# Seven products of quarters for layer 0's output projection, from the second image on

## The chip, the cores and the metric

The kernel runs on one core of a Trainium2 chip. A core has a matrix engine (TensorE, PE in the profile, with the weight loads listed apart as PEld), a vector engine (VectorE, DVE), a scalar engine (ScalarE, ACT), a general engine (GpSimd, POOL) and a sync engine (SyncE, SP) that issues most DMA transfers. Each engine works through its own instructions in the order in which they were written out, and waits where an operand is not ready. Matrix results land in PSUM, everything else that is on the chip lies in SBUF, and the rest in DRAM.

The metric is the device time of one execution in microseconds (us). The kernel before takes 2559.91 us, the median of three runs (2559.35 to 2560.78).

## The reference

Two attention layers follow one another on x of shape (8, 512, 32, 32): eight images, 512 channels, 1024 positions. Everything is fp32 outside of what is shown.

```python
# layer 0, per image, T = 1024
h = group_norm(x, gn_w, gn_b)                      # 32 groups
qkv = einsum('oc,bct->bot', qkv_w, h) + qkv_b      # 8 heads of 64 channels
q, k, v = fake_quant(q), fake_quant(k), fake_quant(v)   # 8 bits, one range for all images
w = softmax(einsum('bct,bcs->bts', q * scale, k * scale))
a = einsum('bts,bcs->bct', w, v).reshape(b, 512, T)
a = einsum('oc,bct->bot', proj_w, a) + proj_b      # the projection
x1 = x + a
# layer 1, one head of 512 channels, T = 1024
h = group_norm(x1, gn_w, gn_b)
q, k, v = (h^T @ w + bias for w in (wq, wk, wv))
out = softmax(q k^T / sqrt(512)) v
x2 = x1 + out @ wp + bp
```

The line that the change touches is the projection of layer 0: for each image a product of a 512x512 weight with 512x1024 values, then a bias for each output channel and the residual x.

## The kernel before, in words

Channels lie on the 128 partitions in four chunks (`CC = 4`), the 1024 positions in two halves of 512 (`NH = 2`). The eight heads of layer 0 are worked in four pairs.

Up to about 400 us the group norm and the products for q, k and v of all images run, since the ranges for the quantisation cover all of them. From then on two streams are woven together. `attention()` (line 1018) does layer 0's attention for image after image, in units of (image b, pair j, half hf, key tile s): a unit has two score products (`st<-q,k`), an exponential on ACT into a tile `pt` (four buffers, so unit u reuses the buffer of unit u - 4), a cast of it to 16 bit (`two`, by ACT, or by POOL for every fourth), a subtract on DVE that keeps the rest in a second 16-bit tile (`two<-pt,two`), the product with the values (`av<-two,v`, first with the cast part and then with the rest) and the sums of the rows (`sm<-two,ones`). At the end of a pair `finish` copies the products and sums out of PSUM and `divide` scales the values into a tile `ao`, of 128x2x512 for each pair, so four of these make the projection's right-hand side.

The other stream, `others()` (line 1900), does for one image after the other the projection, the second group norm (`norm1`, line 1344) and layer 1 (`layer1`, line 1655). It is one image behind the attention, and each `yield` in it lets the attention go on by four units. So while layer 1 of image b runs, the attention of image b + 1 runs beside it and ends shortly before the projection that needs it; the projection and norm of image b + 1 stand inside layer 1 of image b, behind the fourth of the seven products of its last `o_run` (line 1540; `first()` at line 1764 calls `project(b + 1, score_bank)`). For the last image no attention is left to run beside.

The order on DVE and ACT is written out by a planner. The class `InOrder` (line 53) wraps both engines. Its `do` puts an operation down at once; its `later` puts one on a list of chores with a cost, a time when it is ready and a time when it is due; `fill` takes chores from the list as long as they fit before a given time by the planner's own clock, the one that is ready first going first; and `settle` takes all of a kind at once. A `dma_start` on ACT adds 0.5 us to the planner's clock. Each instruction is tied behind the one put down before it on its engine. All operations of DVE and ACT are therefore recorded at line 91 (`call` in `InOrder`), and all matmuls at line 209 (`mm`), so that the tiles' names tell them apart: `pj` is the projection's PSUM tile, `wp` its weight, `h` the residual x that becomes x1, `vec` the biases.

Before each projection `load_wp` (line 1265) loads its weight of 1 MB in one DMA and `load_x2` loads x in two, all issued on ACT's queue near the end of layer 1 of the image before (lines 1756 and 1757). `project` (line 1296) then takes, in each half and for each of four output chunks, four matmuls of 128x512 into one PSUM bank; DVE evicts each bank with one operation that adds bias and residual, SP stores x1, and `bn_stats` and `bn_aggr` gather the statistics of the second group norm (chores "pj", forced at the end by `settle("pj")`). Between the halves there is one `yield`, in which the attention goes on.

Most of the products of layer 1 are already done by `seven` (line 1393): two matrices of 2x2 quarters are multiplied with seven products of quarters in place of eight, after sums and differences of the quarters were made on both sides. Here a product of quarters is four matmuls of 128x256, and its result goes with others into two PSUM banks that are used in turn. The sums of the weights' quarters are made once, those of the values for each image and half. Tiles of layer 1 that the change borrows are `vsum` (sums of the value tile's quarters, needed by `o<-g,vsum`), and `v` (`vt`, the value tile itself, 128x8x512).

Of the kernel before, what the change touches and what calls it, by code (L numbers as in the profile page):

```python
# [9 lines left out]
F32 = mybir.dt.float32  # L10
# [8 lines left out]
P = 128  # L19
# [39 lines left out]
def attn_pair_kernel(  # L59
# [97 lines left out]
    def elements(n):  # L157

        return 0.21 + n * 0.957e-3

    def chore():
        dve.fill(pe.t)

    def awaits(t):

        pe.t = max(pe.t, t + 0.1)
# [140 lines left out]
    with ExitStack() as fast:  # L307
# [710 lines left out]
        def attention():  # L1018
# [138 lines left out]
            def finish(b, j, hf, u):  # L1157

                nm = f"{b}_{j}"
                if hf == 0:  # L1160
                    if b:
                        settle("ao")
                    ao[b, j] = aop.tile([P, NH, 512], F32, tag="ao", name=f"ao_{nm}")
                    if b == 0 and j % 2 == 1:
                        rss[b, j] = kept_u[:, 0:2].rearrange("p h k n -> p h (k n)")
                    else:
                        rss[b, j] = l1p.tile([P, NH, 512], F32, tag="rs", name=f"rs_{nm}")
                aot, rs = ao[b, j], rss[b, j]
                act.do(0.6, lambda: act.copy(aot[:, hf, :], avs.pop((b, j, hf))))
                act.do(0.6, lambda: act.copy(rs[:, hf, :], sms.pop((b, j, hf))))  # L1170
                if hf == 0:
                    return
                del rss[b, j]
                n = b * PAIRS + j

                apart = small.tile([P, 2, 16], F32, tag="apart", name=f"apart_{nm}")
                for w in range(2):
                    nc.sync.dma_start(
                        apart[:, w, :],
                        rs[2 * w * QUAD : 2 * (w + 1) * QUAD : QUAD].rearrange(  # L1180
                            "r h (p k) -> r h p k", k=16
                        ),
                    )

                def divide():
                    dve.scalar_tensor_tensor(aot, aot, scl[:, 2:3], rs, ALU.mult, ALU.mult)

                def spread():
                    r = rcs[:, n * 16 : (n + 1) * 16]
                    dve.tensor_add(r, apart[:, 0, :], apart[:, 1, :])  # L1190
                    dve.reciprocal(r, r)
                    nc.sync.dma_start(rs_d[n].rearrange("r (p k) -> (r p) k", k=16), r)
                    for i, r in enumerate(HALF):
                        nc.sync.dma_start(
                            rs[r], rs_d[n][2 * i : 2 * i + 2, :].partition_broadcast(CH)
                        )
                    if InOrder.planned:
                        dve.later("ao", elements(1100), divide, dve.t + 7.0, 20.0)
                    else:
                        dealt.append((u + (20 if j < PAIRS - 1 else 13), "ao", divide))  # L1200

                if InOrder.planned:
                    dve.later("ao", 0.4, spread, pe.t + 5.0, 8.0)
                else:
                    dealt.append((u + (12 if j < PAIRS - 1 else 7), "ao", spread))
# [58 lines left out]
                dma(xts[b][:, :, bass.ts(hf, 512)], x_v[b, :, :, bass.ts(hf, 512)])  # L1264

        def load_wp(b, dma):
            wps[b] = l2p.tile([P, CC, C], F32, tag="sums", name=f"wp0_{b}")
            dma(wps[b], w_sq[WP0])

        def load_first(u):  # L1270

# [21 lines left out]
            for t, src in zip(wm_tiles(b), wm_d):  # L1293
                act.dma_start(t, src)

        def project(b, bank=bank):

            settle("ao")  # L1300
            st, mvs[b] = stat_tiles(CC, f"b{b}")
            wp0 = wps.pop(b)
            for hf in range(NH):
                for oc in range(CC):
                    ps = bank(f"pj_{b}_{hf}_{oc}")
                    for cc in range(CC):
                        mm(
                            ps, lhsT=wp0[:, cc, bass.ts(oc, P)], rhs=ao[b, cc][:, hf, :],
                            start=(cc == 0), stop=(cc == CC - 1),
                        )  # L1310
                    xx = xts[b][:, oc, bass.ts(hf, 512)]

                    def evict():
                        dve.scalar_tensor_tensor(
                            xx, ps, vec[:, V_PB0 + oc : V_PB0 + oc + 1], xx, ALU.add, ALU.add
                        )
                        nc.sync.dma_start(x1_d[b][oc // 2][hf][:, oc % 2, :], xx)

                    def stats(oc=oc, hf=hf, xx=xx):
                        dve.bn_stats(st[:, oc, hf, :], xx)  # L1320
                        if hf == NH - 1:
                            aggregate(mvs[b], st, oc)

                    dve.do(elements(550), evict)
                    dve.later("pj", 0.62 + 0.2 * hf, stats, within=4.0)
                    chore()
                if hf + 1 < NH:
                    yield -1
            settle("pj")
            for k in [k for k in ao if k[0] == b]:  # L1330
                del ao[k]
# [12 lines left out]
        def norm1(b, bank=bank):  # L1344

            def at(cc, hf):
                return xts[b][:, cc, bass.ts(hf, 512)]

            def put(hf, cost, work):
                if hf == 0:  # L1350
                    dve.do(cost, work)
                else:
                    dve.later("h", cost, work, within=27.0)

            def put_sum(hf, i, work):
                if hf == 0:
                    dve.later("t4" if i == 3 else "t", elements(512), work, within=10.0 + 2.0 * i)
                else:
                    put(hf, elements(512), work)

            for n, _ in enumerate(norm_steps(
                at, at, V_GN1W, bank, f"b{b}", put=put, mv=mvs[b]
            )):
                if n == 2:
                    sums[b] = l2p.tile(
                        [P, 3, NH, CC // 2, 256], F32, tag="sums", name=f"sums2_{b}"
                    )
                    for hf in range(NH):
                        h11, h12, h21, h22 = quarters(b, hf)
                        t1, t2, t4 = (sums[b][:, i, hf] for i in range(3))  # L1370
                        for i, args in enumerate((
                            (t1, h12, h11), (t2, h22, t1), (h12, h22, h12), (t4, h21, t2)
                        )):
                            put_sum(hf, i, lambda args=args: tt(*args, ALU.subtract))
                yield
# [14 lines left out]
            dve.later("o", 0.25, spread, pe.t + 4.0, 5.0)  # L1390
            return rs

        def seven(nm, pairs, keep, whole, add, bank=bank):

            nonlocal turn
            turn ^= 1  # L1400
            x, y = (bank(f"{nm}_{i}").rearrange("p (t n) -> p t n", t=2) for i in range(2))

            def product(n, ps, start):
                left, right = pairs[n]
                k = left.shape[1]
                for t in range(2):
                    for i in range(k):
                        mm(
                            ps[:, t, :], lhsT=left[:, i, bass.ts(t, P)], rhs=right[:, i, :],
                            start=start and t == 0 and i == 0, stop=(i == k - 1),  # L1410
                            skip_group_check=True,
                        )

            work = (
                (0, x, True, keep, 0), (1, y, True, add, 0), (2, x, False, keep, 1),
                (3, y, True, keep, 2), (4, x, False, add, 2), (6, y, False, add, 1),
                (5, x, False, whole, None),
            )
            for i, (n, ps, start, out, m) in enumerate(work):
                awaits(free[(i + turn) % 2])  # L1420
                product(n, ps, start)
                free[(i + turn) % 2] = out(ps) if m is None else out(m, ps)
                yield i + 1

        free = [0.0, 0.0]
        turn = 0

        def slots(gq):
# [226 lines left out]
        def layer1(b, steps):  # L1655
# [46 lines left out]
            for hf in range(NH):  # L1702
# [52 lines left out]
                if last and b + 1 < B:  # L1755
                    load_wp(b + 1, act.dma_start)
                    load_x2(b + 1, act.dma_start)
                if done >= B:
                    load_x1(b, hf, 0, 1, rx, aop)
                settle("v")  # L1760
                between = [lambda: iter((1,)), lambda: iter(()), lambda: iter(())]
                if b + 1 < B and last:

                    def first():
                        nonlocal ahead
                        yield -1
                        yield from project(b + 1, score_bank)
                        yield 2
                        ahead = norm1(b + 1, score_bank)
                        next(ahead)  # L1770
# [534 lines left out]
```

## Time and profile before

| what | value |
|---|---|
| median of three runs | 2559.91 us |
| the profiled execution | 2559.32 us |
| its span | 2557.2 us |
| granted TensorE clock | 0.999 |
| busy: PE | 2515.9 us, 98% |
| busy: DVE | 1897.6 us, 74% |
| busy: ACT | 1346.5 us, 53% |
| busy: POOL | 186.0 us, 7% |
| matmul records of the projection | 512 |
| first start of a projection, images 0 to 7 | 692.7, 930.72, 1171.0, 1411.2, 1651.4, 1891.9, 2132.3, 2362.4 us |

A line of the profile's groups gives the line of the kernel, the engine, the operation, the output tile and the tiles read, their shapes, the number of instructions, their busy time and mean duration in ns, and after the bar the idle time of the engine just before them with what ended most of it. A line of the timeline gives the start, the duration, the engine, and the same names; a group of equal instructions that follow one another is one line, `x32` being their number, and what stands in square brackets is how long the engine was idle before and what it waited for. The durations of matmuls are modelled and overlap: 32 matmuls that follow one another are read from the start of the first to the start of what comes next on PE. One fp32 matmul is recorded twice. A queue such as ACTq or SPq lists the issue of DMA transfers. The chain of work that ended last is followed back from the last instruction; its line gives the share of the span that each engine holds of it.

### The profile page before, as it was taken

To read this page: it belongs to the slowest core of one execution; us is meant where nothing else is said; L and a number is where in the kernel's file an instruction comes from. 1 tells how busy PE (TensorE), PEld (TensorE's weight loads), DVE (VectorE), ACT (ScalarE), POOL (GpSimd) and SP (SyncE) were. 2 spreads that over 40 slices of the span, in tenths; PEclk is the share of its full clock that TensorE was granted. 3 is DMA by queue.
4 is the path that set the end of the run, shared out by engine and by line. 5 is a ranking of instruction groups with operands and counts; after the bars stand their busy time and mean duration, and the time that the engine had idled before them with its cause. 6 is when DMAs were issued, how large, how long until landed. Compare 5 with 4: busy or idle time off the path is not lost.

```text
span 2557.2 us, 38727 instructions
## 1 busy us (share of the span) xinstructions
PE 2515.9 (98%) x15670; PEld 1746.2 (68%) x15670; DVE 1897.6 (74%) x2747; ACT 1346.5 (53%) x1685; POOL 186.0 (7%) x167
## 2 busy tenths in 40 slices
PE   8999999999999999999999999999999999999998
PEld 4788888873357756775777577667756775777787
DVE  7887776668887778777877787777778777885544
ACT  3332223319857655665666466656655665664121
POOL 0000000001100001000100100010101000100000
PEclk9999999999999999999999999999999999999999
DMA  4533333236622232223313222322232123212211
GB/s 168 177 142 125 131 124 122 109 131 162 162 88 63 79 116 85 58 74 122 98 57 100 92 79 78 110 92 63 79 112 88 55 71 128 96 42 80 87 38 39
DMA packets 160717, 250.70 MB, mean 98 GB/s; under 512 B 27152, under 2 KB 93712, under 8 KB 159120
## 3 DMA queue, kind: packets, MB, share of 16 engines
q1 hardware_dynamic: 125792, 182.81, 21.6%
q10 hardware_dynamic: 30560, 57.71, 6.5%
q0 software_dynamic: 4176, 7.60, 1.7%
q8 instruction: 125, 2.05, 0.3%
q14 instruction: 64, 0.52, 0.1%
HBM read 153.64 MB, written 86.28 MB: 94 GB/s over the span
## 4 chain that ended last, share of the span: by engine, by line
PE 85%; DVE 5%; ACT 2%; issue 1%; DMA 1%; POOL 0%; SPq 0%; ACTq 0%; DVEq 0%
PE s L209 15%; PE o L209 13%; PE qkps L209 12%; PE pj L209 8%; PE av L209 8%; PE v2ps L209 7%; PE vps L209 6%; PE g L209 6%; PE st L209 4%; PE sm L209 3%; DVE two L91 2%; ACT pt L91 1%; PE fold L209 1%; DVE h L91 1%; DVE acc L91 0%
## 5 line engine op out<-in xcount | busy, mean ns | idle before, releaser
L91 ACT ACTIVATE pt<-st,esc 128x1024 f32<-128x1024 f32 x467 | 496.4, 1114 | 332.1 <-PE st L209 317.6
L91 DVE TENSOR_TENSOR two<-pt,two 128x1024 f16<-128x1024 f32 x467 | 561.5, 1216 | 131.0 <-POOL two L1092 100.7
L91 ACT CAST two<-pt 128x1024 f16<-128x1024 f32 x346 | 350.8, 1055 | 6.9 <-ACT p L91 5.1
L1092 POOL CAST two<-pt 128x1024 f16<-128x1024 f32 x112 | 146.0, 1304 | 1409.4 <-PE sm L209 746.3
L209 PE MATMUL av<-two,v 128*32 128x512 f16 x3968 | 245.9, 381 | 2.5 <-DVE two L91 2.1
L209 PE MATMUL s<-g,h 128*128 128x256 f32 x1024 | 233.4, 380 | 0.0
L209 PE MATMUL pj<-ao,wp 128*128 128x512 f32 x512 | 224.1, 595 | 0.6 <-DVE h L91 0.6
L209 PEld LDWEIGHTS s<-g,h 128*128 128x128 f32 x1024 | 192.9, 190 | 31.0 <-issue 4.3
L91 ACT ACTIVATE u_ring<-qkps,qkbt 128x512 f32<-128x512 f32 x89 | 60.9, 685 | 243.8 <-PE qkps L209 219.3
L209 PEld LDWEIGHTS <-v 128*32 128x32 f16 x3968 | 91.8, 96 | 140.0 <-issue 66.7
L209 PEld LDWEIGHTS pj<-ao,wp 128*128 128x128 f32 x512 | 96.0, 190 | 122.5 <-issue 110.8
L209 PE MATMUL s<-g,sums 128*128 128x256 f32 x768 | 178.4, 381 | 0.2 <-DVE p L91 0.2
L209 PE MATMUL o<-p,v 128*128 128x256 f32 x768 | 175.2, 382 | 1.0 <-DVE p L91 1.0
L209 PE MATMUL st<-q,k 64*128 64x512 bf16 x1024 | 163.4, 382 | 11.9 <-ACT pt L91 7.5
L209 PEld LDWEIGHTS o<-p,v 128*128 128x128 f32 x768 | 144.3, 190 | 27.1 <-issue 5.7
L209 PEld LDWEIGHTS s<-g,sums 128*128 128x128 f32 x768 | 144.7, 190 | 24.2 <-issue 4.6
L209 PE MATMUL sm<-two,ones 128*32 128x512 f16 x1984 | 136.0, 379 | 0.0
L209 PEld LDWEIGHTS <-k 64*128 64x128 bf16 x1024 | 34.8, 94 | 143.8 <-issue 142.2
L209 PE MATMUL qkps<-half,w_high 128*128 128x512 f32 x480 | 132.4, 398 | 0.0
L209 PE MATMUL qkps<-half,w_mix 128*128 128x512 f32 x480 | 130.6, 394 | 1.0 <-DVE half L91 1.0
L209 PE MATMUL qkps<-half,w_low 128*128 128x512 f32 x480 | 130.5, 394 | 0.0
L209 PE MATMUL v2ps<-wm,h 128*128 128x256 f32 x512 | 119.9, 383 | 1.9 <-ACT g L91 1.3
(226 smaller groups left out, 3902.2 us busy)
## 6 DMA issues: line engine op xcount, KB each, us to landing
rs<-rs_d SPq DMA_DIRECT2D x76, 256.0 KB
x<-in_x_dram SPq DMA_DIRECT2D x32, 512.0 KB
q_d<-wa SPq DMA_DIRECT2D x32, 512.0 KB
k_d<-wa SPq DMA_DIRECT2D x32, 512.0 KB
v_d<-v_ring SPq DMA_DIRECT2D x32, 512.0 KB
raw<-q_d SPq DMA_DIRECT2D x32, 512.0 KB
raw<-k_d SPq DMA_DIRECT2D x32, 512.0 KB
x_d<-h SPq DMA_DIRECT2D x64, 256.0 KB
```

What stands on the lines that cost most here:

```text
L91: ins = self.latest = op(*args, **kw).ins
L209: ins = nc.tensor.matmul(ps, lhsT=lhsT, rhs=rhs, **kw).ins
L1092: copy(two[:, 0], pt)
```

## The change

Image 0 keeps the old projection. For it, `combine_wp` makes the four sums of the weight's quarters with four DVE operations of 128x512 in the `vsum` buffer, and SP stores them to a DRAM tile `wp_d` of 1 MB.

From image 1 on `project` hands over to `project_seven`. In each half it takes seven products of quarters, 28 matmuls of 128x256, into one pair of PSUM banks. DVE adds each product to its quarter of x in place (seven operations of 128x2x256, in place of four evictions), and takes four sums of 128x256 in place in the `ao` tiles for the values' side; two more sums of 128x2x256 go into part of `vt` once for both halves (`second`), and two are made in place when the second pair's `divide` is done (`first_sums`). The bias is added to x ahead of the projection, by four ACT operations of 128x1024 (`add_bias`, chores "xb"). The weight now comes in three DMAs (0.5, 0.25 and 0.75 MB), the last from `wp_d`; the fourth sum comes by a DMA of 0.25 MB into part of `vt` when the projection starts. x1 is stored in eight pieces of 128x2x256 for each image. `seven` gets the argument `alone`, with which it keeps a record of bank times of its own, and takes lists of tiles as the right-hand side. The statistics of a half are put on the list after its sixth and seventh product.

```diff
                 def divide():
                     dve.scalar_tensor_tensor(aot, aot, scl[:, 2:3], rs, ALU.mult, ALU.mult)
+                    if b and j == 1:
+                        first_sums(b)
...
         def load_wp(b, dma):
-            wps[b] = l2p.tile([P, CC, C], F32, tag="sums", name=f"wp0_{b}")
-            dma(wps[b], w_sq[WP0])
+            wps[b] = w = l2p.tile([P, 6, CC // 2, C // 2], F32, tag="sums", name=f"wp0_{b}")
+            dma(w[:, 0:2].rearrange("p i k n -> p (i k) n"), w_sq[WP0][:, :, 0 : C // 2])
+            dma(w[:, 2], w_sq[WP0][:, CC // 2 :, C // 2 :])
+            dma(w[:, 3:6], wp_d[:, 0:3])
...
-        def project(b, bank=bank):
+        wp_d = dram.tile([P, 4, CC // 2, C // 2], F32, tag="wp", name="wp_d")
+
+        def combine_wp():
+            wc = l2p.tile([P, 3, NT // 2, 256], F32, tag="vsum", name="wp_combined").rearrange(
+                "p a (s k) n -> p (a s) k n", k=2
+            )
+            a11, a12, a21, a22 = (
+                wps[0][:, k * CC // 2 : (k + 1) * CC // 2, m * 256 : (m + 1) * 256]
+                for m in range(2) for k in range(2)
+            )
+            s2, s3, s1, s4 = (wc[:, i] for i in range(4))
+            for args in (
+                (s1, a21, a22, ALU.add), (s2, s1, a11, ALU.subtract),
+                (s3, a11, a21, ALU.subtract), (s4, a12, s2, ALU.subtract),
+            ):
+                dve.later("wc", elements(512), lambda args=args: tt(*args), within=20.0)
+            dve.later("wc", 0.0, lambda: nc.sync.dma_start(wp_d, wc[:, 0:4]), within=20.0)
+
+        def add_bias(b):
+            for cc in range(CC):
+                act.later("xb", 1.05, lambda cc=cc: act.activation(
+                    xts[b][:, cc, :], xts[b][:, cc, :], AF.Identity,
+                    bias=vec[:, V_PB0 + cc : V_PB0 + cc + 1],
+                ), pe.t + 17.0, 24.0)
+
+        def first_sums(b):
+            for cc in range(CC // 2):
+                h = ao[b, cc]
+                dve.later("at", elements(512), lambda h=h: tt(
+                    h[:, :, 256:512], h[:, :, 256:512], h[:, :, 0:256], ALU.subtract
+                ), within=30.0)
+
+        def project_seven(b, room):
+            settle("at")
             settle("ao")
+            act.settle("xb")
+            st, mvs[b] = stat_tiles(CC, f"b{b}")
+            w = wps.pop(b)
+            a11, a12, a22, s2, s3, s1 = (w[:, i] for i in range(6))
+            t2 = room[:, 0 : NT // 2, 0:256].rearrange("p (k h) n -> p k h n", h=NH)
+            s4 = room[:, NT // 2 : NT // 2 + 2, 0:256]
+            act.dma_start(s4, wp_d[:, 3])
+            left, right = slice(0, 256), slice(256, 512)
+            def second(k):
+                tt(t2[:, k], ao[b, 2 + k][:, :, right], ao[b, k][:, :, right], ALU.subtract)
+            for k in range(2):
+                dve.do(elements(512), lambda k=k: second(k))
+            for hf in range(NH):
...
+                def into(q, row, col, full, hf=hf):
+                    def add(ps):
+                        there = dve.do(elements(512), lambda: tt(q, ps, q, ALU.add))
+                        if full is not None:
+                            nc.sync.dma_start(x1_d[b][row][hf][:, :, col * 256 : (col + 1) * 256], q)
+                        return there
+                    return add
...
+                for step in seven(
+                    f"pj_{b}_{hf}",
+                    ((a11, h11), (a12, h21), (s2, th), (s3, h11), (s1, t1), (s4, h22), (a22, h21)),
+                    lambda n, ps: keeps[n](ps), into(q12, 0, 1, 1), lambda n, ps: adds[n](ps),
+                    lambda _: next(banks), True,
+                ):
+                    if step in (1, 2):
+                        for k in range(2):
+                            h = (h11, h21)[step - 1][k]
+                            args = (h, th[k], h) if step == 1 else (h, h, th[k])
+                            dve.do(elements(256), lambda args=args: tt(*args, ALU.subtract))
+                    for oc in {6: (2, 3), 7: (0, 1)}.get(step, ()):
+                        dve.later("pj", 0.62 + 0.2 * hf, lambda oc=oc, stats=stats: stats(oc), within=4.0)
+                    chore()
+                if hf + 1 < NH:
+                    yield -1
+            settle("pj")
...
+        def project(b, room=None):
+            if b:
+                yield from project_seven(b, room)
+                return
+            settle("ao")
+            combine_wp()
...
-        def seven(nm, pairs, keep, whole, add, bank=bank):
+        def seven(nm, pairs, keep, whole, add, bank=bank, alone=False):
             nonlocal turn
-            turn ^= 1
+            turn ^= not alone
+            free, side = ([0.0, 0.0], 0) if alone else (busy, turn)
...
-                            ps[:, t, :], lhsT=left[:, i, bass.ts(t, P)], rhs=right[:, i, :],
+                            ps[:, t, :], lhsT=left[:, i, bass.ts(t, P)],
+                            rhs=right[i] if type(right) is list else right[:, i, :],
...
                 if last and b + 1 < B:
                     load_wp(b + 1, act.dma_start)
                     load_x2(b + 1, act.dma_start)
+                    add_bias(b + 1)
...
-                        yield from project(b + 1, score_bank)
+                        yield from project(b + 1, vt)
```

More of the change, by code (lines that the diff above doesn't have):

```diff
@@ new lines, in project_seven, with stats @@
+        def project_seven(b, room):
+            settle("at")
+            settle("ao")
+            act.settle("xb")
[11 more added lines that the diff above has]
+            for hf in range(NH):
+                h11, t1, h21, h22 = (
+                    [ao[b, c + k][:, hf, n] for k in range(2)] for c in (0, 2) for n in (left, right)
+                )
+                th = [t2[:, k, hf] for k in range(2)]
+                q11, q12, q21, q22 = quarters(b, hf)
+                at = pair_ps(f"pj_{b}_{hf}")
+                banks = iter((at[:, 0, :], at[:, 1, :]))
+                def into(q, row, col, full, hf=hf):
[5 more added lines that the diff above has]
+                    return add
+                def stats(oc, hf=hf):
+                    dve.bn_stats(st[:, oc, hf, :], xts[b][:, oc, bass.ts(hf, 512)])
+                    if hf == NH - 1:
+                        aggregate(mvs[b], st, oc)
+                keeps = [into(q, *at_, None) for q, at_ in ((q11, (0, 0)), (q21, (1, 0)), (q22, (1, 1)))]
+                adds = [into(q, *at_, 1) for q, at_ in ((q11, (0, 0)), (q21, (1, 0)), (q22, (1, 1)))]
+                for step in seven(
[15 more added lines that the diff above has]
+            settle("pj")
+            for k in [k for k in ao if k[0] == b]:
+                del ao[k]
@@ L1364, in norm1 @@
                 if n == 2:
+                    if b == 0:
+                        settle("wc")
                     sums[b] = l2p.tile(
@@ L1419, in seven @@
             for i, (n, ps, start, out, m) in enumerate(work):
-                awaits(free[(i + turn) % 2])
+                if not alone:
+                    side = turn
+                awaits(free[(i + side) % 2])
                 product(n, ps, start)
-                free[(i + turn) % 2] = out(ps) if m is None else out(m, ps)
+                free[(i + side) % 2] = out(ps) if m is None else out(m, ps)
                 yield i + 1
-        free = [0.0, 0.0]
+        busy = [0.0, 0.0]
         turn = 0
```

## The prediction

> **What bounds the kernel now.** I read the page first: busy shares, the chain of work that ended last, the costliest groups.
>
> ```profile
> PE 2515.9 (98%) x15670; PEld 1746.2 (68%) x15670; DVE 1897.6 (74%) x2747; ACT 1346.5 (53%) x1685; POOL 186.0 (7%) x167
> PE 85%; DVE 5%; ACT 2%; issue 1%; DMA 1%; POOL 0%; SPq 0%; ACTq 0%; DVEq 0%
> L209 PE MATMUL pj<-ao,wp 128*128 128x512 f32 x512 | 224.1, 595 | 0.6 <-DVE h L91 0.6
> L209 PE MATMUL s<-g,h 128*128 128x256 f32 x1024 | 233.4, 380 | 0.0
> ```
>
> TensorE is the bound: 98% busy at a granted clock of 0.999, and it waited only 0.6 us for the projection's results in the whole run. Removed products are worth their full time only while nothing new makes PE wait. So I read one image by the timeline (start, us, engine, operation). Images 1 to 6 repeat within 0.01 us, counted from each one's project start; I show image 2, whose project starts at 930.72. First the project's first half, and six products of quarters of layer 1, of the shape the change will use:
>
> ```profile
> 930.72 14.00 PE L209 MATMUL pj<-ao,wp 128*128 128x512 f32 x32
> 944.65 0.39 PE L209 MATMUL st<-q,k 64*128 64x512 bf16 x2
> ...
> 981.86 3.72 PE L209 MATMUL g<-h,wa 128*128 128x256 f32 x16
> 985.42 1.89 PE L209 MATMUL g<-sums,wa 128*128 128x256 f32 x8
> 987.15 1.98 PE L209 MATMUL g<-h,wa 128*128 128x256 f32 x8
> 988.96 3.62 PE L209 MATMUL g<-sums,wa 128*128 128x256 f32 x16
> 992.51 0.61 PE L209 MATMUL st<-q,k 64*128 64x512 bf16 x4
> ```
>
> A half of the projection holds PE from 930.72 to 944.65, 13.93 us for 32 records (each fp32 matmul is recorded twice). Six products hold it from 981.86 to 992.51: 10.65 us, 1.775 each.
>
> Next, what runs ahead of the project, where its loads are issued:
>
> ```profile
> 909.20 1.04 ACT L91 CAST two<-pt 128x1024 f16<-128x1024 f32 x1 [0.84 <-ACT p L91]
> 910.27 1.23 DVE L91 TENSOR_TENSOR two<-pt,two 128x1024 f16<-128x1024 f32 x1 [0.56 <-ACT two L91]
> 911.21 0.58 ACT L91 COPY kept_u<-o 128x512 f32<-128x512 f32 x1 [0.97 <-PE o L209]
> 911.64 1.91 PE L209 MATMUL av<-two,v 128*32 128x512 f16 x32
> 911.69 2.14 ACT L91 ACTIVATE pt<-st,esc 128x1024 f32<-128x1024 f32 x2
> ```
>
> The cast of score tile 3 and its subtract end at 911.50, just before the 32 value matmuls, whose last four need that subtract. Last, the end of the second half:
>
> ```profile
> 955.78 7.46 PE L209 MATMUL pj<-ao,wp 128*128 128x512 f32 x17
> 963.17 1.05 PE L209 MATMUL av<-two,v 128*32 128x512 f16 x16
> 963.28 0.75 DVE L91 SCALAR_TENSOR_TENSOR h<-pj,vec,h 128x512 f32<-128x512 f32 x1 [0.71 <-PE pj L209]
> 964.06 0.69 DVE L91 BATCH_NORM_STATS2 gst_b<-h 128x6 f32<-128x512 f32 x1
> 964.58 2.12 ACT L91 ACTIVATE pt<-st,esc 128x1024 f32<-128x1024 f32 x2 [11.91 <-PE st L209]
> 964.79 0.21 DVE L91 BATCH_NORM_AGGREGATE gmv_b<-gst_b 128x2 f32<-128x12 f32 x1
> 965.13 1.04 PE L209 MATMUL av<-two,v 128*32 128x512 f16 x16
> 966.53 0.62 PE L209 MATMUL st<-q,k 64*128 64x512 bf16 x4
> ```
>
> One eviction, one statistics pair, and no subtract stand here: the subtracts of tiles 6, 7, 0 and 1 ran between the evictions, while PE multiplied.
>
> **Products.** Seven products replace 16 matmuls of 512 columns: 7 x 1.775 = 12.43 us for 13.93, 1.50 less. Seven images of two halves: 14 x 1.50 = -21.0 us. By bare record pitch (1.72 a product) the half is 12.2 and the sum -24.
>
> [...] In the rows a record of 256 columns takes 1.775 / 8 = 0.222 us and one of 512 takes 13.93 / 32 = 0.435; the rows decide.
>
> **Late cast, images 1 to 6.** Loading takes five DMA issues on ACT's queue where there were three, and the planner charges each 0.5 us. By the two orders, the cast of tile 3, before directly behind the issues, now stands behind the kept_u copy and the exponential of tile 6, although ACT is idle from 910.24 to 911.21. Copy ends 911.79, exponential 912.8, cast 913.85, subtract 915.05. PE reaches its use at 911.64 + 28/32 of the group = 913.17: it waits 1.9 us. Behind the cast on ACT stands the exponential of tile 7, which reuses tile 3's buffer and waits for the same subtract; the casts of 4, 5 and 7 follow it, 2.4 late, and the next score pair is late by no more than PE already is. On DVE the subtracts of 6, 4, 5 and 7 queue behind this one and shift with PE, whose next use of them is the value group after the following o products. Bounds: 0 if ACT runs earlier than I read, 2.4 if the exponential binds. 6 x 1.9 = +11.4.
>
> **Within the halves.** Each product's add (0.69, the row of a 128x512 sum) is through 0.8 us after its product, and its bank is wanted 1.775 after: nothing. The in-place 128x256 sums (0.44 by the row x<-kept_u,ob,x of 0.87 for two) fit beside. Behind the first half's last add now stand subtracts 3, 4 and 5 (1.2 each) and three statistics. Subtract 3 is through 2.1 us after the half, its use comes about 3 us after; subtract 4 at 3.3 frees the exponential whose end the second half awaits at 4.4, for 4.6 before: nothing, bound +0.3 an image.
>
> **Tail, images 1 to 6.** From PE's turnover (963.17 in before): last add +0.11 to 0.80, three statistics pairs at 0.86 to 3.4, subtract 6 to 4.6, subtract 7 to 5.8. The exponentials that reuse those two buffers end at about 5.8 and 7.0, and PE's fourth score tile waits for the second. Before, that exponential ended at 966.70, 3.5 after turnover. PE loses 3.4 (by subtract 7 alone, against its use at 2.75, 3.1). Bounds 2.5 and 3.8. 6 x 3.4 = +20.4. DVE has 2.78 idle before the o add at 970.84, so the lag ends there.
>
> **Image 7** has no attention beside it: -3.0, plus 0.25 as four bias additions (1.05 each) follow ACT's copy at 2362.61 and delay the first adds, plus 0.1 for the end: -2.65.
>
> **Image 0** gets the four combining sums. One (0.69) comes ahead of the first eviction, where PE already waits (0.65 us): +0.6, bounds 0 and 1. The others fit DVE gaps. The 1 MB store on SP has some 200 us.
>
> **Costed at nothing, with cover.** Biases: two in ACT's idle 3.48 us ahead of its copy at 926.33, two in its 10.34 ahead of 945.08. The s4 load is issued near 936 and wanted by the last product near 943; 256 KB (rs from rs_d) takes 3.8 us. Without cover each us late costs 6. The extra 0.5 MB: the loads landed by 920.5 at some 390 GB/s, so 1.3 more, 921.8; the first bias wants the x tile at 922.9, with ACT's copy and four exponentials queued behind it (later with PE's lag); doubled time for the 1 KB pieces (768 KB, 2 us) would eat that margin. The two sums of t2 (930.8 to 932.2) precede the first add, due 932.6; if late, 0.1. First sums (2 x 0.69) take the place of a vsum sum of 1.2 that is wanted 30 us later. POOL's order is unchanged. SP: eight x1 stores of another shape, read 40 us on; the output store of tile (0,0), put 17 us later, still ends before its buffer's load at 969.17.
>
> **Sum**, against the profiled execution's 2559.32 (span 2557.2): images 1 to 6 each -3.0 + 1.9 + 3.4 = +2.3, 13.8; image 7 -2.65; image 0 +0.6: +11.75, 2571.1. The median of the runs is 0.6 above that execution: 2571.7; I say 2571.5. Less than 0.2% (5.1 us, about what a measurement here can tell) is 2554.8 to 2565.0.
>
> **Rivals.**
> 1. The tail costs nothing (the other side): 2571.7 - 20.4 = 2551.3, faster. It needs DVE through subtract 7 by 2.7 us after the last product instead of 5.8: three statistics pairs would have to run ahead of the last add. The written order speaks against it. Price per image 3.4; it decides from 1.9 recovered per image. 0.06.
> 2. The late cast does not bind: 2571.7 - 11.4 = 2560.3, same. For it: ACT has 0.97 idle there, and order alone makes the delay. Against: copy, exponential, cast and subtract are rows in series. 0.13.
> 3. Neither binds: 2539.9, 0.03.
> 4. The loads come late and a bias holds ACT's exponentials: the margin is 1.1 us plus PE's lag of 1.9; each us beyond it adds 6: about 2578 at 1 us, 2584 at 2. For it: 768 KB in 1 KB pieces. Against: the DMA rows near 390 GB/s. 0.08.
>
> My forecast has 0.70, its own range 2564 to 2577 by its bounds. The range of eight in ten takes in rival 2 and the near end of 4: 2558 to 2578. Slower: 0.70 less the forecast's low edge 0.04, plus 0.08: 0.74; same 0.17; faster 0.09.
>
> **What would show it.** After's pj group of 256 columns, a half in 12.4 us; ACT's cast behind the exponential some 17 us ahead of each project, and PE idle 1.9 there for DVE's two; PE idle 3 us or more behind the second half, ended by DVE two or ACT pt; image 7's block 2.7 shorter. Wrong if DVE runs its tail in other places, or a product exceeds 1.99 us, where seven equal the old half.

## The result and the profile after

The changed kernel takes 2675.81 us (median of four runs, 2674.7 to 2679.0) beside 2560.35 us for the kernel before: a ratio of 1.0454 (1.0435 to 1.0472), 115 us slower. I had forecast 2571.5. The direction was right, the size was wrong by a factor of ten: slower by 11 was forecast, slower by 115 was measured. The profiled execution has a span of 2674.5 us, 117.3 more than before.

First the page of the changed kernel, the lines that answer to those shown of before:

```profile
PE 2533.5 (95%) x16006; PEld 1810.0 (68%) x16006; DVE 1967.1 (74%) x2877; ACT 1378.8 (52%) x1713; POOL 188.5 (7%) x167
PE 76%; DVE 12%; issue 3%; ACT 2%; DMA 2%; POOL 1%; ACTq 0%; SPq 0%; DVEq 0%; POOLq 0%
L209 PE MATMUL pj<-ao,wp 128*128 128x256 f32 (+1 forms) x624 | 169.3, 416 | 50.8 <-DVE h L91 50.8
```

PE is down from 98% to 95% busy, and DVE holds 12% of the chain instead of 5%. The rows of the projection used to have 0.6 us of idle time ahead of them; now one of their three groups alone has 50.8, all ended by DVE's `h`, which is the add of a product to x. The list of PE's waits (what waited, for what: us in total, times, the longest) names the two that grew:

```profile
PE pj L209 <- DVE h L91: 72.7, 85, 3.6
PE av L209 <- DVE two L91: 22.8, 23, 2.0
```

85 waits: one ahead of each of the last six products in 14 halves of seven, and one in image 0. The timeline of the first half of image 1 (the project that starts at 930.72 in before; the prediction calls it image 2 where it shows it, and it is the first of its images 1 to 6) shows what a half looks like:

```profile
932.90 1.99 PE L209 MATMUL pj<-ao,wp 128*128 128x256 f32 x8
935.68 1.99 PE L209 MATMUL pj<-ao,wp 128*128 128x256 f32 x8 [0.79 <-DVE h L91]
938.46 1.99 PE L209 MATMUL pj<-v,wp 128*128 128x256 f32 x8 [0.79 <-DVE h L91]
...
949.64 1.99 PE L209 MATMUL pj<-ao,v 128*128 128x256 f32 x8 [0.78 <-DVE h L91]
951.57 0.39 PE L209 MATMUL st<-q,k 64*128 64x512 bf16 x2
```

and DVE beside it:

```profile
934.93 0.69 DVE L91 TENSOR_TENSOR h<-pj,h 128x512 f32<-128x512 f32 x1 [0.67 <-PE pj L209]
935.54 0.75 DVE L91 TENSOR_TENSOR ao<-v,ao 128x256 f32<-128x256 f32 x2
937.71 0.69 DVE L91 TENSOR_TENSOR h<-pj,h 128x512 f32<-128x512 f32 x1 [1.42 <-PE pj L209]
```

The products start every 2.78 us, not every 1.775. Each starts 0.06 us after the end of the add of the product just ahead of it (934.93 + 0.69 = 935.62, then 935.68). But two banks are used in turn, so the add of the product before the last is all that the next should need. DVE is no reason for it: it waited 1.42 us for PE in turn. PE and DVE take turns where they should work side by side. The half lasts 951.57 - 932.90 = 18.67 us, 4.74 more than the 13.93 before, where 12.43 was forecast.

### The profile page after: what moved, and what is told of

The parts are those of the page before. It is cut to its first block, busy times and chain, and to the rows that moved or that the text cites. A ratio compares the mean times of both kernels' runs of the same rounds, so it can differ in the third digit from the quotient of the medians.

```text
span 2674.5 us, 39680 instructions
## 1 busy us (share of the span) xinstructions
PE 2533.5 (95%) x16006; PEld 1810.0 (68%) x16006; DVE 1967.1 (74%) x2877; ACT 1378.8 (52%) x1713; POOL 188.5 (7%) x167
## 4 chain that ended last, share of the span: by engine, by line
PE 76%; DVE 12%; issue 3%; ACT 2%; DMA 2%; POOL 1%; ACTq 0%; SPq 0%; DVEq 0%; POOLq 0%
PE s L209 15%; PE o L209 12%; PE qkps L209 12%; PE pj L209 7%; PE v2ps L209 7%; PE vps L209 6%; PE av L209 6%; PE g L209 5%; DVE two L91 4%; DVE h L91 4%; PE st L209 3%; PE sm L209 3%; ACT pt L91 1%; DVE gst_b L91 1%; DMA wp<-in_w_sq_dram 1%
## 5 line engine op out<-in xcount | busy, mean ns | idle before, releaser
L91 DVE TENSOR_TENSOR two<-pt,two 128x1024 f16<-128x1024 f32 x467 | 569.1, 1239 | 127.9 <-POOL two L1092 69.2
L209 PE MATMUL av<-two,v 128*32 128x512 f16 x3968 | 251.4, 382 | 27.1 <-DVE two L91 22.8
L209 PE MATMUL pj<-ao,wp 128*128 128x256 f32 (+1 forms) x624 | 169.3, 416 | 50.8 <-DVE h L91 50.8
L209 PEld LDWEIGHTS pj<-ao,wp 128*128 128x128 f32 x624 | 113.7, 191 | 105.4 <-DVE h L91 74.1
L91 DVE TENSOR_TENSOR h<-pj,h 128x512 f32<-128x512 f32 x98 | 67.6, 690 | 126.2 <-PE pj L209 124.1
```

The costliest lines, as they stand in the source:

```text
L91: ins = self.latest = op(*args, **kw).ins
L209: ins = nc.tensor.matmul(ps, lhsT=lhsT, rhs=rhs, **kw).ins
```

## The experiments

### Where the waits of the products come from

In the changed kernel the two banks of a half are the two halves of one PSUM tile of two banks, `at`. In layer 1 the same function `seven` gets two tiles of its own for its two banks. The list of PE's instructions in the built programs shows what that does, for the first two products of image 2 (first matmul of each):

```
changed kernel   pj_2_0   <-ao_2_0,wp0_2   128x256 [waits DMAHW0, Activation]
                 pj_2_0   <-ao_2_2,wp0_2   128x256 [waits DVE]
two tiles        pj_2_0_0 <-ao_2_0,wp0_2   128x256 [waits DMAHW0, Activation]
                 pj_2_0_1 <-ao_2_2,wp0_2   128x256 [waits Activation]
```

The wait is one that the program sets: with one tile, the second product, which writes the other bank, waits for DVE at its first matmul; with two tiles it waits there only for ACT, which used the buffer before, and the wait for the first product's add stands on the third product, which writes the same bank again. **e1_two_tiles** makes this edit and no other (`score_bank` hands out the first bank of a two-bank tile, so the half now holds both buffers of the scores' tiles, where `at` held one):

```diff
-                at = pair_ps(f"pj_{b}_{hf}")
-                banks = iter((at[:, 0, :], at[:, 1, :]))
...
-                    lambda _: next(banks), True,
+                    score_bank, True,
```

> The changed kernel, with the two banks of a half's seven products in two PSUM tiles of their own instead of the two halves of one tile. Theory A (each product waits for the add of the product ahead of it because both banks lie in one tile, for which the program orders any write behind any read): the idle 0.79 us ahead of each product goes, a half takes 12.4 to 12.6 us instead of 18.7, some 6.2 x 14 = 87 us go, and with the late cast (+11.4), the tail (4.4 an image, 5.8 in two of them, as in the changed kernel) and the first image (+0.4) left, the time is 2575 to 2590. Rival B (the adds or the sums of quarters in place on DVE are too slow, so products wait for DVE whatever tile they write): the waits stay, 2660 to 2680.

Measured: 2583.41 us, ratio to before 1.0093 (1.0076 to 1.0110). 92.4 us of the 115.5 are gone. The timeline of the same half with two tiles has no wait left in it:

```profile
933.49 3.72 PE L209 MATMUL pj<-ao,wp 128*128 128x256 f32 x16
937.04 1.89 PE L209 MATMUL pj<-v,wp 128*128 128x256 f32 x8
938.77 5.34 PE L209 MATMUL pj<-ao,wp 128*128 128x256 f32 x24
943.95 1.89 PE L209 MATMUL pj<-ao,v 128*128 128x256 f32 x8
945.77 0.39 PE L209 MATMUL st<-q,k 64*128 64x512 bf16 x2
```

945.77 - 933.49 = 12.28 us for seven products, 1.754 each. The adds and the in-place sums are the same in both, so rival B falls: DVE is fast enough. That it is the shared tile, whatever is multiplied, is tested from the other side in **e2_one_tile_before**, which puts the old projection's four groups on the two halves of one tile:

```diff
+                at = pair_ps(f"pj_{b}_{hf}") if b else None
                 for oc in range(CC):
-                    ps = bank(f"pj_{b}_{hf}_{oc}")
+                    ps = at[:, oc % 2, :] if b else bank(f"pj_{b}_{hf}_{oc}")
```

> The kernel before, its projection unchanged but for the banks: from image 1 on the four groups of a half write the two halves of one PSUM tile in turn, where each had a tile of its own. Theory A (one tile alone puts each group behind the eviction of the group ahead, whatever the products are): a wait of about 1.0 us (0.75 eviction and some 0.3 around it) ahead of three groups a half, 14 halves: +42 us, 2595 to 2610. Rival (two banks of one tile are harmless, and it was the seven products' own pattern that made the waits): 2560 within 3.

Measured: 2607.84 us, ratio 1.0186 (1.0170 to 1.0202), +48 us. A half now reads:

```profile
931.64 3.70 PE L209 MATMUL pj<-ao,wp 128*128 128x512 f32 x8
...
940.73 3.70 PE L209 MATMUL pj<-ao,wp 128*128 128x512 f32 x8 [0.84 <-DVE h L91]
945.28 3.70 PE L209 MATMUL pj<-ao,wp 128*128 128x512 f32 x8 [0.84 <-DVE h L91]
```

and the list of PE's waits has 42 of them, which is three in each of 14 halves (image 0 has none in this run):

```profile
PE pj L209 <- DVE h L91: 36.6, 42, 1.2
```

A group starts every 4.55 us where 13.93 / 4 = 3.48 was the pace before: 1.07 each, 42 x 1.07 = 45 us. The harm needs no seven products; it needs one tile with two users.

### The late cast

**e3_late_cast_before** takes the late cast alone, in the kernel before. The planner is told that the load issues cost 1.0 us more, which is what two more issues are charged:

```diff
                     load_x2(b + 1, act.dma_start)
+                    act.t += 1.0
```

> The kernel before, with the planner's clock for ACT put forward by 1.0 us after the load issues, as two more issues do: the cast of tile 3 moves behind the copy and the exponential of tile 6, and nothing else changes on ACT. Theory: PE waits 1.9 us (2.4 by the exponential of tile 7) in images 1 to 6: +11 to +15 us, 2571 to 2575. Rival: the lag is taken up by PE's later waits on ACT: less than +4.

Measured: 2571.17 us, ratio 1.0044 (1.0028 to 1.0060), +11.3 us. Its value matmuls ahead of image 1's projection and ACT beside them:

```profile
912.64 1.48 PE L209 MATMUL av<-two,v 128*32 128x512 f16 x24
914.80 0.40 PE L209 MATMUL av<-two,v 128*32 128x512 f16 x4 [0.68 <-ACT two L91]
916.06 0.40 PE L209 MATMUL av<-two,v 128*32 128x512 f16 x4 [0.86 <-DVE two L91]
...
912.21 0.59 ACT L91 COPY kept_u<-o 128x512 f32<-128x512 f32 x1 [2.86 <-PE o L209]
912.70 1.12 ACT L91 ACTIVATE pt<-st,esc 128x1024 f32<-128x1024 f32 x1
913.70 1.04 ACT L91 CAST two<-pt 128x1024 f16<-128x1024 f32 x1
```

The group of 32 takes from 912.64 to 916.27, 3.63 us, where it took 1.74 before, from 911.64 to the next group's start:

```profile
913.38 1.04 PE L209 MATMUL sm<-two,ones 128*32 128x512 f16 x16
```

1.89 is lost, while ACT sat idle for 2.86 us just ahead. The edit changes the order of the instructions and nothing else.

**e4_cast_first** takes the late cast out of the changed kernel with two tiles, by setting the planner's clock back:

```diff
                     load_x2(b + 1, act.dma_start)
+                    act.t -= 1.0
                     add_bias(b + 1)
```

> The two tiles of e1_two_tiles, and the planner's clock for ACT set back by 1.0 us after the load issues, so that tile 3's cast stands directly behind the issues again. Theory: the late cast costs PE 1.9 us in each of images 1 to 6, so this is 11.4 us faster than e1_two_tiles (10 to 14). Rival: the five issues themselves hold ACT, and the order alone changes nothing: within 2 us of e1_two_tiles.

Measured: 2570.18 us, ratio 1.0040 (1.0026 to 1.0054), 13.2 us less than e1_two_tiles. The group of 32 reads `911.72` to the next group's `913.45` there, 1.73 us.

### The tail behind the second half

In e1_two_tiles the second half of image 1 ends at 962.97, and then:

```profile
967.36 0.62 PE L209 MATMUL av<-two,v 128*32 128x512 f16 x8 [2.04 <-DVE two L91]
968.49 0.47 PE L209 MATMUL av<-two,v 128*32 128x512 f16 x4 [0.52 <-DVE two L91]
968.71 1.11 PE L209 MATMUL sm<-two,ones 128*32 128x512 f16 x8
969.75 1.03 PE L209 MATMUL st<-q,k 64*128 64x512 bf16 x4
970.72 4.39 PE L209 MATMUL o<-g,vsum 128*128 128x256 f32 x16
974.94 0.28 PE L209 MATMUL gps_b<-gmv_b,gavg 128*128 128x4 f32 x2
```

Before, the same stretch ended so:

```profile
967.08 3.72 PE L209 MATMUL o<-g,vsum 128*128 128x256 f32 x16
970.64 0.28 PE L209 MATMUL gps_b<-gmv_b,gavg 128*128 128x4 f32 x2
```

From 962.97 to the group norm's product at 974.94 it is 11.97 us, against 970.64 - 963.17 = 7.47 before: 4.5 lost. 2.04 and 0.52 of it are waits for the subtracts of tiles 6 and 7; the sums, score and o groups then take 1.11, 1.03 and 4.39 instead of 0.60, 0.62 and 3.72. Behind the same two waits in the changed kernel, where the sums and the score group take 1.09 and 1.03, the granted clock was 0.50 (below). **e5_tail** leaves the two tiles and lets the statistics wait until the subtracts are through:

```diff
                 if hf + 1 < NH:
                     yield -1
-            settle("pj")
+            if b == B - 1:
+                settle("pj")
...
                     def more():
+                        settle("pj")
                         next(ahead)
```

> The two tiles of e1_two_tiles, and the statistics of the last half no longer forced at the end of the projection but one step later, so that on DVE the subtracts of tiles 6, 7, 0 and 1 stand ahead of three statistics pairs. Theory: PE's wait behind the second half falls from 4.4 us (with the lower clock after it) to 0.9: some 21 to 25 us faster than e1_two_tiles, 2555 to 2566. Rival: DVE is short of time there in any order, and the wait comes back later at the group norm: less than 8 us faster than e1_two_tiles.

Measured: 2566.06 us, ratio 1.0023 (1.0013 to 1.0032), 17.3 us less than e1_two_tiles, short of the 21 to 25 expected. Of the waits behind the half, one of 0.34 us is left, and the sums and the o group behind them take 0.62 and 3.72 again. From the start of image 1's project to that of image 7's the profiled span is 18.1 us shorter (2366.25 - 934.01 against 2383.81 - 933.49), 3.0 an image where 3.5 was the least expected: the stretch behind the half still takes 8.77 us (963.50 to 972.27), 1.3 more than before. The rest of the miss lies outside the part that was edited: image 1 starts 0.5 us later, behind a stretch at a granted clock of 0.50 (689.92 to 693.34), and image 7 takes 2.4 us longer.

**e6_all** has all three edits.

> All three edits together (two tiles, cast first, statistics later). Theory: the three costs add up, so this is 32 to 37 us faster than e1_two_tiles: 2543 to 2555, faster than the kernel before. Rival: the costs hide one another and at most the larger of the two gains is left: no faster than e5_tail.

Measured: 2554.56 us, ratio 0.9979 (0.9969 to 0.9988), 28.9 us less than e1_two_tiles where 32 to 37 were expected, and the first version faster than the kernel before, by 0.2%. The costs nearly add up (13.2 + 17.3 = 30.5), so the rival falls, but the expected 2543 to 2555 was met only at its edge. Images 1 to 6 are together 8.8 us shorter than before (2355.61 - 932.71 against 2362.41 - 930.72), of the 19.8 that their twelve halves save: 1.3 an image is still lost behind the second half and 0.3 between the halves. Image 7 lost more than it saved.

### Image 7, and a version that beats both

In e6_all image 7, from the start of its project to the end of the span, takes 2553.4 - 2355.61 = 197.8 us, against 194.8 before, where I had forecast 2.65 less. ACT and PE at its start:

```profile
2358.45 1.15 ACT L91 ACTIVATE h<-h,vec 128x1024 f32<-128x1024 f32 x1 [2.05 <-DMA h<-in_x_dram]
...
2355.61 3.62 PE L209 MATMUL pj<-ao,wp 128*128 128x256 f32 x16
2361.42 3.68 PE L209 MATMUL pj<-v,wp 128*128 128x256 f32 x8 [2.19 <-DVE h L91]
2364.93 5.34 PE L209 MATMUL pj<-ao,wp 128*128 128x256 f32 x24
```

The bias waits for x, which is loaded behind 1.5 MB of weights; the project of image 7 starts 14 us after the load issues (2341.45 to 2355.61), where no attention runs beside it, instead of 23 (909.75 to 932.71 in image 1). PE waits 2.19 us, and the third product then takes 3.5 us (to 2364.93) instead of 1.75. **e7_x_first** is e6_all with the two loads exchanged:

```diff
-                    load_wp(b + 1, act.dma_start)
                     load_x2(b + 1, act.dma_start)
+                    load_wp(b + 1, act.dma_start)
```

> The kernel of e6_all, with x loaded ahead of the weight. In e6_all's last image the bias waits 2.05 us for x, the first add 2.2 us for the bias, and PE then runs a product at half clock. Theory: x lands some 4 us earlier, the wait and the slow product go: 3 to 5 us faster than e6_all, 2549 to 2552. Rival: the weight is then late instead, and PE waits for it: no gain.

Measured: 2551.3 us, ratio 0.9967 (0.9955 to 0.9979), 3.3 us less. The biases run from 2356.89, when ACT's copy ends, and the second and third product stand without a wait. Image 7 is 4.4 us shorter (2549.6 - 2356.21 = 193.4), and its two halves take 24.47 us instead of 27.47 before, the 3.0 that were forecast; images 1 to 6 are together 1.8 longer than in e6_all, which was not traced.

**e8_subtract_inside** puts one subtract by hand between the adds of the second half:

```diff
+                    if hf and step == 4:
+                        i = next((i for i, c in enumerate(dve.chores) if c[0] == "sum"), None)
+                        if i is not None:
+                            dve.begin(i)
                     for oc in {6: (2, 3), 7: (0, 1)}.get(step, ()):
```

> The kernel of e7_x_first, with the subtract of tile 6 put by hand behind the fourth add of the second half. Theory: behind the half only one subtract stands ahead of PE's use, the remaining wait of 0.3 to 0.9 us in images 1 to 6 goes: 2 to 5 us faster than e7_x_first. Rival: the subtract makes the fifth and sixth product wait for DVE instead: no gain, or slower.

Measured: 2543.52 us, ratio 0.9937 (0.9923 to 0.9951): 16 us faster than the kernel before and 132 faster than the changed one. It gained 7.8 over e7_x_first, more than the 2 to 5 expected. In the profiled executions the gain is 8.8: 7.6 in images 1 to 6, 1.27 an image, and 1.3 ahead of image 1 (930.17 instead of 931.51), which the edit does not touch: the granted clock of e7_x_first is 0.58 from 690 to 692 us and 0.56 from 692 to 694, and 1.00 in e8_subtract_inside. Behind the second half of image 1 nothing waits any more:

```profile
957.84 1.89 PE L209 MATMUL pj<-ao,v 128*128 128x256 f32 x8
959.66 1.05 PE L209 MATMUL av<-two,v 128*32 128x512 f16 x16
960.64 0.61 PE L209 MATMUL st<-q,k 64*128 64x512 bf16 x4
...
961.62 1.04 PE L209 MATMUL av<-two,v 128*32 128x512 f16 x16
962.48 0.60 PE L209 MATMUL sm<-two,ones 128*32 128x512 f16 x8
...
963.57 3.72 PE L209 MATMUL o<-g,vsum 128*128 128x256 f32 x16
```

and the products between which the subtract stands still follow one another without a gap (952.66 to 957.84 is three products in 5.18 us). The rival of that run falls too.

## Why the prediction was wrong

**The step that failed** is "Within the halves": "Each product's add ... is through 0.8 us after its product, and its bank is wanted 1.775 after: nothing." The first half of the sentence is nearly right: by the pace of e1_two_tiles the first product's place on PE ends at 932.90 + 1.754 = 934.65 and its add at 935.62, 0.97 us later. The second half is wrong: the next product wanted the whole tile, and at once. What was put at nothing cost 6.4 to 6.7 us a half (18.67 and 18.97 against 12.28). I took "two banks in turn" from the text of the change and priced the waits by the pattern of layer 1, where two tiles are used; the difference between two tiles and two halves of one stood in two lines of the changed kernel that the shortened diff above does not print (`at = pair_ps(...)` and `banks = iter((at[:, 0, :], at[:, 1, :]))`) and in the built program's waits. So no rival held it either: none of the four was a product that waits for the add of the product ahead. "Wrong if ... a product exceeds 1.99 us, where seven equal the old half" was the right alarm; a product took 2.78. That the direction came out right is only in part the merit of the forecast: 92.4 of the 115.5 us come from the tile, which it did not hold, and e1_two_tiles, without that, is still 23 us slower than before by the late cast, the tail and image 7.

In numbers, the changed kernel's profiled span less that of before, 117.3 us, against the forecast's 11.8:

| term | forecast | the profile of the changed kernel | tested by |
|---|---|---|---|
| 14 halves | -21.0 | half 1 is 4.74 longer than before, half 2 5.04 (956.48 to 975.45): 7 x 9.78 = +68.5 | e1, e2 |
| between the halves, images 1 to 6 | 0, bound +0.3 an image | 951.57 to 956.48 is 4.91, 4.59 before: +1.9 | not tested apart |
| late cast, images 1 to 6 | +11.4 | 911.92 to 915.55 for the value group, 1.89 each: +11.3 | e3, e4 |
| tail, images 1 to 6 | +20.4 | 975.45 to 987.36 is 11.91, +4.44; 1.36 more in images 2 and 5: +29.4 | e5 |
| image 7 besides its halves | +0.35 | 210.8 us instead of 194.8, less 9.78: +6.2 | e7, for 4.1 of it |
| image 0 | +0.6 | PE's wait ahead of its third group 1.28 instead of 0.65: +0.6; its project starts 0.3 earlier | not tested apart |

These sum to 117.6, for the 117.3 measured. Before, the second half of image 1 started here, 4.59 us after the first half's end at 944.65:

```profile
949.24 14.00 PE L209 MATMUL pj<-ao,wp 128*128 128x512 f32 x32
```

**The products** themselves were priced right. With the wait gone, e1_two_tiles shows 12.28 us a half against 12.43 forecast and 12.2 as the bound (a bound that the pitch given with it, 1.72 a product, does not make: 7 x 1.72 = 12.04). The changed kernel's half takes 18.67, but what it takes beyond 12.28 lies between the products, as e1_two_tiles shows. Per column a record of 256 costs 0.7 to 1.9% more in these fp32 rows than one of 512 (1.754 or 1.775 / 8 against half of 13.93 / 32).

**The late cast** was right to 0.1 us a time, in the changed kernel, alone in the kernel before (+11.3) and taken out again (-13.2).

**The tail** was right in kind (the waits are ended by the subtracts of tiles 6 and 7, in the order that was read; it is the value matmuls that wait, and not the score tile that the sum had waiting for an exponential) and too small in size: 3.4 forecast, 4.4 to 5.8 measured. The two waits are 2.04 and 0.52 us, less than 3.4; what the sum did not hold is the lower clock behind them (0.50 for 3.4 us behind image 1 and for 6.8 us behind image 2), by which the sums, score and o groups cost 0.5, 0.4 and 0.5 to 1.8 us more than before.

**Image 7** was wrong: the load's margin was worked out for images 1 to 6 only. There rival 4 did not happen; in image 7 its mechanism did, and cost what PE lost by waiting (3.64 us in the changed kernel) and by the product behind it, at a granted clock of 0.50 from 2470 to 2472 us (3.60 instead of 1.89):

```profile
2469.23 3.60 PE L209 MATMUL pj<-ao,wp 128*128 128x256 f32 x8 [3.64 <-DVE h L91]
```

This is 4.1 of the 6.2. The other 2.1, forecast as 0.1, stand behind all of the work: from the end of DVE's last operation to the end of the span it is 6.0 us before and 8.0 in the changed kernel, 7.4 to 8.5 in the six other versions with the seven products and 5.9 to 6.0 in the two others with the old projection. Why is open.

**The forecast without the tile** would have been 2571.7 against 2583.41 for e1_two_tiles: 11.7 us too low, mostly from the tail (4.5 instead of 3.4, 6.6 for six images) and from image 7 (1.4 longer than before instead of 2.65 shorter: 4.0); what the halves saved beyond the forecast, 0.15 each, was lost again between them.

## What to carry to other kernels

Buffers that are to be used in turn must be tiles of their own for the program that sets the waits (the shared tile cost 6.4 to 6.7 us a half here): before pricing a hand-over between two engines, read the wait that stands on the first instruction of each step in the built program, not the addresses. A saving on the bound engine is worth only what the order on the other engines lets through: here the same seven products make the kernel 4.5% slower or 0.6% faster, by one PSUM tile, one cast behind two load issues, four statistics, the order of the loads and one subtract. And a margin that holds in the repeated part has to be worked out again for the last round, where the cover is missing.

## What the runs showed of the hardware

**In the changed kernel a short stall cost a second time, through the clock.** Windows of the changed kernel behind image 1's second half (stretch, its length, busy time of PE, PEld, DVE, ACT, POOL, the granted clock, DMA share, GB/s):

```profile
980.00:981.00 1.00, 0.48 (x12) 0.12 (x8) 1.00 (x2) 0.99 (x1) 0.00 (x0) 0.95 0.00 0
981.00:982.00 1.00, 1.00 (x12) 0.30 (x11) 1.00 (x2) 0.99 (x1) 0.95 (x1) 0.50 0.00 0
...
983.00:984.00 1.00, 1.00 (x4) 0.57 (x3) 1.00 (x2) 0.97 (x1) 0.00 (x0) 0.50 0.00 0
984.00:985.00 1.00, 1.00 (x6) 0.84 (x5) 1.00 (x2) 0.73 (x2) 0.00 (x0) 0.84 0.00 0
```

After PE had waited 2.04 and 0.52 us the granted clock was 0.50 from about 980.9 (0.95 in that window is a tenth of it at half) to 984.32. That is 3.4 us. Behind image 2 it lasted twice as long:

```profile
1236.00:1237.00 1.00, 0.51 (x8) 0.21 (x8) 1.00 (x2) 0.47 (x1) 0.00 (x0) 0.95 0.00 0
...
1243.00:1244.00 1.00, 1.00 (x4) 0.79 (x4) 0.00 (x0) 1.00 (x2) 0.00 (x0) 0.64 0.42 128
```

From 1236.9 to 1243.72 it is 6.8 us, with PE busy for most of it; images 2 and 5 took 1.36 us longer for it than their neighbours. The same stall of 2.04 us stands behind every second half of images 1 to 6 of the changed kernel, and the half clock followed it six times of six: 3.4 us behind images 1, 3, 4 and 6, 6.8 us behind images 2 and 5. A single wait of about 1.6 us ahead of image 0's project was followed by it in e5_tail (0.50 from 689.92 to 693.34), e6_all (0.50 from 690 to 694) and e7_x_first (0.58 and 0.56 in the two stretches of 2 us from 690 to 694), and not in the kernel before, the changed kernel, e1_two_tiles and e8_subtract_inside (1.00 from 688 to 696). The twelve waits of 0.78 to 1.16 us inside the two halves of image 1's changed projection left the clock at 1.00.

So the length of a wait alone does not tell whether the half clock follows it: the one of 1.58 us ahead of image 0's project was followed by it in e7_x_first and not in the kernel before and e1_two_tiles. What decides it was not shown.
